# A transformer block on one core: background work of ScalarE and VectorE is put elsewhere, with six smaller edits

## The chip, the cores and the metric

The kernel runs on one core of one Trainium2 chip. The metric is the time of one execution on the device in microseconds (us). An engine is called by the profile's short name where a row is meant: PE is TensorE (matmuls), PEld its weight loads, DVE VectorE, ACT ScalarE, POOL GpSimd, SP SyncE. Engines run in parallel, each through its own list of instructions in order, and wait for each other by semaphores. A transfer is issued from the list of SP, ACT or POOL.

## The reference

One block of a transformer on x of 2048 tokens by 1024 features, all float32. `layernorm` has no weights.

```python
def attn(h):                       # h = layernorm(x)
    q, k, v = (h @ w.T + b for w, b in ((wq, bq), (wk, bk), (wv, bv)))
    q, k, v -> (tokens, 32 heads, 32)
    scores = einsum('shd,std->sht', q, k) / sqrt(32)     # heads of ONE token against each other
    return einsum('sht,std->shd', softmax(scores), v)

def ffn(h):                        # h = layernorm(x)
    dq1, dq2, dq3 = (nf4_quant_dequant(w) for w in (w1, w2, w3))   # blocks of 64, 16 levels
    return (silu(h @ dq1.T) * (h @ dq2.T)) @ dq3.T                 # 1024 -> 2752 -> 1024

x = x + attn(layernorm(x))
x = x + ffn(layernorm(x))
```

`nf4_quant_dequant` divides each block of 64 weights by its largest magnitude, replaces every value by the nearest of 16 levels, and multiplies by the magnitude again.

## The kernel before

**Products.** Every large product is a two by two block product done with seven multiplications instead of eight (Strassen's scheme in Winograd's form). A multiplication is `mm4`: four matmuls of 128x128 by 128x512, which the profile shows as eight rows. The scheme needs sums and differences of the blocks (`S1` to `S4` of the one side, `T1` to `T4` of the other), which VectorE makes, and reads a PSUM bank several times while it still grows: `copied` and the copies of `Unit` are ScalarE's copies of such a bank, and the next multiplication into the bank must wait for the copy.

**Stages.** The queries' sweep goes over eight pairs of token blocks (128 tokens each): `load_x`, `normed_x`, transposes into `A` (plain order) and `V` (order for the values) by TensorE with two ScalarE copies per PSUM tile, `products`, then `qk_T` adds the bias. The A and V operands are kept in DRAM. In the first pair the weight combinations T1 to T4 are made on the chip as the blocks land. The keys' sweep multiplies the same operands by the keys' weights and does `attend` (scores and softmax). The values' sweep multiplies by the values' weights and does `gather` (context), `residual` (adds x and normalizes) and `keep_T` (transposes the result, forms its sums and stores them). Then comes the feed-forward part: `Unit`s (gate and up projection of one block of 128 hidden features, for one of two halves of the tokens) in groups of four, and after each group `down7`, the sum over the group's hidden features. `down7` copies each PSUM bank with ScalarE (`acc`) and adds it to `x1d` in DRAM with accumulating transfers of GpSimd. The last groups go through `down`.

**The background.** The quantization of w1, w2, w3 is 64 jobs, a generator (`background`) that runs beside all of this. A job loads a weight block `wn`, finds the blocks' maxima (`absmax`, which also divides: `scaled` with `rc`), walks through 15 steps that build `r` (twelve of them are an `sg` on ScalarE, L242, and an operation on VectorE, L243; two buffers of `sg`), multiplies by the maxima (`scaled` with `wa`), and is transposed by TensorE, copied by ScalarE (`finish`, L162) and stored (`wd`). Jobs of kind "1" and "2" are the up side, "3" the down side. `scaled` on ScalarE is one small instruction for each of 16 blocks of 64 columns.

**What sets the order.** The main program calls `advance(n)` to emit n background pieces, `flush` to emit a finished job's transposes, and, in the feed-forward part, `spent(us)`, which emits `us * RATE` pieces (RATE is 0.69 a microsecond). `until(kind, c)` emits whatever is missing of a job that is needed now. TensorE's order is exactly that of the program. The other engines' order is made by a scheduler from the emitted instructions, unless `tc.issue_after` puts an instruction behind another. `hook["scale"]` says which engine does the last `scaled` of a job: in the sweeps "ACT"; from the feed-forward part on "DVE", which means VectorE for even jobs and ScalarE for odd ones.

Of the kernel before, what the change touches and what calls it, by code (L numbers as in the profile page):

```python
# [69 lines left out]
def preln_block_kernel(  # L70
# [41 lines left out]

    def mean_var(pool, src, dst):
        st = pool.tile([P, 2, 6], FP, tag="st", name="st")
        for j in range(2):
            nc.vector.bn_stats(st[:, j, :], src[:, ts(j, 512)])
        nc.vector.bn_aggr(dst, st.rearrange("p a b -> p (a b)"))
# [74 lines left out]
    def scaled(dst, src, by, nb):  # L192

        for n in range(nb):
            nc.scalar.mul(dst[:, ts(n, BLOCK)], src[:, ts(n, BLOCK)], by[:, n : n + 1])  # L195
# [4 lines left out]
    def absmax(kind, c, wn):  # L200

        w = width(kind, c)
        nb = w // BLOCK
        v = wn[:, :w]
        am = fs.tile([P, 16], FP, tag="am", name="am")
        rc = fs.tile([P, 16], FP, tag="rc", name="rc")[:, :nb]
        nc.vector.tensor_reduce(  # L207
            am[:, :nb],
            v.rearrange("p (b e) -> p b e", e=BLOCK),
            AX.X,  # L210
            ALU.max,
            apply_absolute_value=True,
        )
        nc.vector.scalar_tensor_tensor(rc, am[:, :nb], 0.0, am[:, :nb], ALU.is_equal, ALU.add)
        nc.vector.reciprocal(rc, rc)  # L215
        scaled(v, v, rc, nb)
        return am

    def background():
# [4 lines left out]
        for n, (kind, c) in enumerate(jobs):  # L224
# [7 lines left out]
            for i, (side, edge, code) in enumerate(STEPS):  # L232
# [6 lines left out]
                else:  # L239
                    t = dqp.tile([P, E], FP, tag="sg", name="sg")[:, :w]  # L240
                    by = BIG if side == "+" else -BIG
                    nc.scalar.activation(t, v, AF.Copy, bias=-edge * by, scale=by)  # L242
# [6 lines left out]
            if hook["scale"] == "ACT" or n % 2:  # L249
                scaled(r, r, wa, w // BLOCK)  # L250
            else:
                r3 = r.rearrange("p (b e) -> p b e", e=BLOCK)
                f = wa[:, : w // BLOCK].unsqueeze(2).to_broadcast([P, w // BLOCK, BLOCK])
                nc.vector.tensor_tensor(r3, r3, f, ALU.mult)
# [68 lines left out]
    def load_bias(b, nm):  # L323
        t = wpool.tile([P, 32], FP, tag=nm, name=nm)
        for g in range(4):
            nc.scalar.dma_start(t[g * 32 : (g + 1) * 32, :], b)
        return t
# [24 lines left out]
    def products(A, fill, used=lambda name: None, apart=None):  # L352
# [7 lines left out]
        def copied(nm, src):  # L360
            t = pair.tile([P, TB], FP, tag=nm, name=nm)
            nc.scalar.copy(t, src)  # L362
            return t
# [21 lines left out]
        if apart is None:  # L385
            mul(z, S4, "B22", False, True)
            nc.scalar.copy(ce[:, 512:], z)
# [68 lines left out]
    xt = {}  # L456

    def load_x(i):
        xt[i] = work.tile([P, E], FP, tag="x", name="xt", bufs=2)
        for n in range(2 if i == 0 else 1):  # L460
            cols = ts(n, TB) if i == 0 else slice(None)
            nc.sync.dma_start(xt[i][:, cols], xf[ts(i, P), cols])
# [3 lines left out]
    def normed_x(i):  # L466
        xn = work.tile([P, E], FP, tag="xn", name="xn", bufs=2)
        return normed(xt.pop(i), xn, opening if i < 2 else None)

    class Inputs:  # L470
# [11 lines left out]
        def transposes(self, j):  # L482
            for half in range(2):
                pt = ps_t.tile([P, 4, P], FP, tag="pt", name="pt")
                for k in range(4):
# [4 lines left out]
                nc.scalar.copy(  # L490
                    v.rearrange("p k (c m) -> p k c m", c=4),
                    pt.rearrange("p k (m c) -> p k c m", c=4),
# [16 lines left out]
    qb_sb, kb_sb, vb_sb = (load_bias(b, nm) for b, nm in ((qb, "qb"), (kb, "kb"), (vb, "vb")))  # L509
# [9 lines left out]
    with tc.issue_after(three(nxt.A, nxt.a21).ins):  # L519
# [40 lines left out]
    for p in range(NP):  # L560
# [11 lines left out]
        def fill(n):  # L572
# [5 lines left out]
            with nullcontext() if p else tc.issue_after(opened):  # L578
                advance(0 if n == 5 else 1)
# [17 lines left out]

    sweep, sweep_at = ExitStack(), ExitStack()
# [85 lines left out]
    def residual(i, at, x1):  # L684
# [6 lines left out]
        nc.vector.tensor_tensor(x1, x1, cx, ALU.add)  # L691
        for n in range(2):
            nc.sync.dma_start(x1d[i][n], x1[:, ts(n, TB)])
        return normed(x1, x1)
# [26 lines left out]
    even = {}  # L721

    def keep_T(i, x1n):

        t = work.tile([P, 2, 4, P], FP, tag=f"xT{i % 2}", name="xT")
        for half in range(2):
# [3 lines left out]
            nc.scalar.copy(t[:, half], pt)  # L730
# [11 lines left out]
        for n in range(4):  # L742
            u[n + 1] = work.tile([P, 4, P], FP, tag="xU", name="xU", bufs=2)
# [4 lines left out]
    for p in range(NP):  # L748
# [9 lines left out]
        def fill(n):  # L758
            if n in (7, 2, 5, 4) and (p, n) != (1, 7):
                part()  # L760
            advance(2 if n == 6 else 1)
# [25 lines left out]
    hook["scale"] = "DVE"  # L787
# [124 lines left out]
    class Unit:  # L912
# [9 lines left out]
        def mul(self, n, dst, start, stop):  # L922
            mm4(dst, self.w[:, self.A[n]], op(self.B[n], self.tbp), start, stop)
            spent(3.43)
# [90 lines left out]
    def down7(g, tbp, sides):  # L1015
# [4 lines left out]
        turn = [0]  # L1020

        def mul(n, dst, q, start, stop):
# [10 lines left out]
            spent(1.71, turn[0] % 2 == 0)  # L1033
# [7 lines left out]
        for first in (0, 2):  # L1041
# [31 lines left out]
            for n, k in opening + [  # L1073
# [3 lines left out]
                p(n, k)  # L1077

# [132 lines left out]
```

## Time and profile before

| | |
|---|---|
| median of 3 runs (lowest, highest) | 2480.15 us (2476.73, 2480.97) |
| the profiled execution, its span | 2484.77 us, 2483.0 us |
| mean granted clock of TensorE | 0.989 |
| busy: PE, DVE, ACT, POOL | 96%, 80%, 65%, 11% |
| 12.4 to 240 us (queries' sweep): PE, DVE, ACT busy of 227.6 us | 211.3, 218.0, 125.9 us |
| 240 to 528 us (keys' sweep): of 288 us | 279.1, 233.5, 137.7 us |
| 528 to 835 us (values' sweep): of 307 us | 283.5, 271.2, 139.9 us |
| a step on ScalarE (L242), on VectorE (L243), 128x1024 | 1060 ns, 1221 ns |
| a small scale on ScalarE (L195), 1032 of them | 341 ns each, 267.5 us together |
| a scale of a whole tile on VectorE (L254) | 1218 ns |

A busy share says how long an engine worked, not whether anybody waited for it. A row of the timeline gives the start, the length, the engine, the line, the operation with its tiles and shape, how many such instructions follow each other, and in brackets how long the engine stood idle before it and what ended that. Eight rows of 128x512 matmuls at full rate print as 3.60 us, though the next eight start 3.43 us later, since a matmul's end overlaps the next one's start. A granted clock under 1.00 in a stretch means that TensorE ran part of it at a lower rate.

### The profile page before, as it was taken

What the parts mean: (1) busy time and instruction counts of PE and PEld (TensorE: products, weight loads), DVE (VectorE), ACT (ScalarE), POOL (GpSimd) and SP (SyncE); (2) the same over time, 40 slices, a digit from 0 to 9 for tenths busy, and PEclk for the clock granted to TensorE, in tenths of its full rate; (3) what the DMA queues carried; (4) which work ended last, traced back from release to release, by engine and by line L of the source; (5) the groups of instructions that cost most, each with busy time, mean ns of one, the idle gap of its engine ahead of it and who ended that gap; (6) DMA issues with size and microseconds to landing.
All of it is one profiled execution on the core that took longest, in us unless ns stands there. A gap on an engine that the chain in (4) does not pass through costs nothing.

```text
span 2483.0 us, 36752 instructions
## 1 busy us (share of the span) xinstructions
PE 2389.2 (96%) x14000; PEld 1117.1 (45%) x14000; DVE 1981.2 (80%) x2211; ACT 1610.2 (65%) x3267; POOL 278.4 (11%) x352
## 2 busy tenths in 40 slices
PE   7999999999899999999999999999999999999998
PEld 4444455545445444444444444444444444444433
DVE  8999688879988597889989899898998988871022
ACT  3566544344554278898887888889889798881200
POOL 0010000000000012030120301203012030020300
PEclk9999999999999999999999999999999999999999
DMA  8888543666669588384883948739577394872983
GB/s 310 301 295 339 214 154 125 228 221 216 198 234 317 196 299 172 126 183 156 310 186 114 185 163 289 181 140 183 165 280 173 132 206 159 278 159 88 173 310 122
DMA packets 179745, 513.90 MB, mean 207 GB/s; under 512 B 16176, under 2 KB 70448, under 8 KB 157168
## 3 DMA queue, kind: packets, MB, share of 16 engines
q1 hardware_dynamic: 138672, 438.08, 48.5%
q0 software_dynamic: 40320, 73.42, 18.4%
q8 instruction: 110, 1.80, 0.3%
q14 instruction: 67, 0.55, 0.1%
q10 hardware_dynamic: 576, 0.05, 0.0%
HBM read 283.69 MB, written 227.80 MB: 206 GB/s over the span
## 4 chain that ended last, share of the span: by engine, by line
issue 25%; ACT 13%; DVE 13%; PE 11%; DMA 6%; POOL 1%; DVEq 0%; POOLq 0%; ACTq 0%
DVE r L243 8%; DMA x1d<-acc 5%; ACT sg L242 4%; PE z L343 4%; ACT wn L195 4%; ACT acc L1037 2%; ACT r L195 2%; PE z L1024 2%; PE q L343 2%; PE po L1104 1%; POOL x1d L1039 1%; PE po L1115 1%; PE y L1024 1%; PE rr L343 1%; ACT wop L162 1%
## 5 line engine op out<-in xcount | busy, mean ns | idle before, releaser
L243 DVE SCALAR_TENSOR_TENSOR r<-sg,r 128x1024 f32<-128x1024 f32 x780 | 945.3, 1213 | 104.1 <-ACT sg L242 72.7
L242 ACT ACTIVATE sg<-wn 128x1024 f32<-128x1024 f32 x780 | 812.6, 1053 | 309.6 <-DVE r L243 294.0
L1039 POOL DMA_DIRECT2D x1d<-acc x280 | 243.0, 887 | 1282.1 <-ACT acc L1037 1138.4
L343 PE MATMUL z<-xB,w 128*128 128x512 f32 x720 | 324.6, 599 | 5.6 <-ACT u L944 3.8
L343 PE MATMUL z<-xT,w 128*128 128x512 f32 x656 | 298.1, 597 | 4.6 <-ACT u L937 4.3
L343 PE MATMUL q<-xT,w 128*128 128x512 f32 x656 | 291.6, 592 | 0.0
L195 ACT ACTIVATE wn<-wn,rc 128x64 f32<-128x64 f32 x1032 | 267.5, 341 | 19.1 <-DVE rc L215 19.1
L1024 PE MATMUL z<-w,h 128*128 128x512 f32 x496 | 233.6, 599 | 9.4 <-ACT acc L1037 6.5
L343 PEld LDWEIGHTS z<-xB,w 128*128 128x128 f32 x720 | 134.6, 191 | 173.6 <-issue 153.0
L343 PEld LDWEIGHTS z<-xT,w 128*128 128x128 f32 x656 | 122.4, 191 | 154.4 <-issue 137.0
L343 PEld LDWEIGHTS q<-xT,w 128*128 128x128 f32 x656 | 123.3, 190 | 149.5 <-issue 146.9
L343 PE MATMUL z<-wT,A 128*128 128x512 f32 x384 | 178.2, 607 | 2.9 <-ACT g L362 2.5
L343 PE MATMUL q<-wT,A 128*128 128x512 f32 x384 | 174.5, 598 | 2.5 <-DVE wT L522 2.5
L343 PE MATMUL z<-wB,A 128*128 128x512 f32 x320 | 153.9, 626 | 12.8 <-ACT u L362 12.8
L195 ACT ACTIVATE r<-r,am 128x64 f32<-128x64 f32 x608 | 154.8, 342 | 14.6 <-DVE r L243 14.3
L1024 PE MATMUL y<-w,h 128*128 128x512 f32 x320 | 150.4, 594 | 1.3 <-DVE h L1003 1.1
L343 PE MATMUL rr<-xB,w 128*128 128x512 f32 x328 | 147.5, 592 | 0.0
L1024 PEld LDWEIGHTS z<-w,h 128*128 128x128 f32 x496 | 92.1, 191 | 121.7 <-issue 96.7
L207 DVE TENSOR_REDUCE am<-wn 128x16 f32<-128x1024 f32 (+1 forms) x65 | 78.3, 1204 | 54.5 <-ACT r L195 54.2
L1037 ACT COPY acc<-z 128x512 f32<-128x512 f32 x160 | 92.9, 580 | 36.9 <-PE z L1024 26.3
L343 PEld LDWEIGHTS q<-wT,A 128*128 128x128 f32 x384 | 72.6, 192 | 90.5 <-issue 85.4
L343 PEld LDWEIGHTS z<-wT,A 128*128 128x128 f32 x384 | 71.5, 193 | 83.0 <-issue 78.1
(132 smaller groups left out, 2585.8 us busy)
## 6 DMA issues: line engine op xcount, KB each, us to landing
x1d<-acc POOLq DMA_DIRECT2D x280, 256.0 KB, 6.4
wd<-wop SPq DMA_DIRECT2D x31, 2048.0 KB, 7.5
w<-wd SPq DMA_DIRECT2D x41, 1280.0 KB, 7.8
wn<-in_w_dram SPq DMA_DIRECT2D x63, 512.0 KB, 5.0
xT<-xdT SPq DMA_DIRECT2D x28, 1024.0 KB, 9.2
xB<-xdB SPq DMA_DIRECT2D x24, 1024.0 KB, 9.0
w<-wd SPq DMA_DIRECT2D x42, 512.0 KB, 5.0
w<-wd SPq DMA_DIRECT2D x10, 1536.0 KB, 7.6
```

The lines of the kernel that those rows point to most:

```text
L162: nc.scalar.copy(o[:q, first + half], pt[:q])
L195: nc.scalar.mul(dst[:, ts(n, BLOCK)], src[:, ts(n, BLOCK)], by[:, n : n + 1])
L207: nc.vector.tensor_reduce(am[:, :nb], v.rearrange("p (b e) -> p b e", e=BLOCK), AX.X, ALU.max, apply_absolute_value=True,)
L242: nc.scalar.activation(t, v, AF.Copy, bias=-edge * by, scale=by)
L243: nc.vector.scalar_tensor_tensor(r, t, code, r, ALU.min, ALU.max)
L343: nc.tensor.matmul(dst, w[:, k, :], xop[:, k, :], start=start and k == 0, stop=stop and k == 3, skip_group_check=True,)
L1024: nc.tensor.matmul(dst, side[n][:, ts(q, P)], w3T[g[2 * m]][:, W3[n]], start=start and m == 0, stop=stop and m == 1, skip_group_check=True,)
L1037: nc.scalar.copy(t, src)
L1039: nc.gpsimd.dma_start(x1d[8 * tbp + 2 * q + j][n], t, accum_op=ALU.add)
L1104: nc.tensor.matmul(po, hs[c][j][:, ts(q, P)], w3T[c][:, ts(n, 512)], start=(c == g[0]), stop=False, skip_group_check=True,)
L1115: nc.tensor.matmul(po, hs[NFULL][r, ts(q, P)], w3T[NFULL][r, ts(n, 512)], start=False, stop=True, skip_group_check=True,)
```

## The change

Seven things change at once.

1. In the queries' and the values' sweep some ScalarE copies are marked, and the background instructions of ScalarE named by `urgent["rule"]` (small scales; in the values' sweep also the steps) are issued behind the last one that is marked. Behind the sweeps the rule is empty.
2. `scaled` takes an engine. In `down7` all scales are VectorE's, those of `absmax` too. Elsewhere in the feed-forward part ("both") the last scale is ScalarE's for even jobs and VectorE's for odd ones.
3. The biases are loaded by GpSimd, behind the normalization of the second token block, instead of by ScalarE at the start.
4. The second pair's tokens are loaded behind the first operand sums, and the first block's normalization comes before the second block's.
5. The residual is formed in the context's tile `cx` and stored from there; the normalized result goes to `x1`.
6. The third buffer of `xU`.
7. The advances: three fewer in the first pair of the queries' sweep, another distribution in the values' sweep, `spent(3.3)` for 3.43 in a unit and `spent(1.85)` for 1.71 in `down7`.

```diff
+    urgent = {"last": None, "rule": ()}
+    def marked(ins):
+        urgent["last"] = ins.ins
+    def behind(kind):
+        last = urgent["last"]
+        return tc.issue_after(last) if last and kind in urgent["rule"] else nullcontext()
...
-    def scaled(dst, src, by, nb):
-        for n in range(nb):
-            nc.scalar.mul(dst[:, ts(n, BLOCK)], src[:, ts(n, BLOCK)], by[:, n : n + 1])
+    def scaled(dst, src, by, nb, engine):
+        if engine == "DVE":
+            d, s = (a.rearrange("p (b e) -> p b e", e=BLOCK) for a in (dst, src))
+            f = by[:, :nb].unsqueeze(2).to_broadcast([P, nb, BLOCK])
+            nc.vector.tensor_tensor(d, s, f, ALU.mult)
+            return
+        with behind("scale"):
+            for n in range(nb):
+                nc.scalar.mul(dst[:, ts(n, BLOCK)], src[:, ts(n, BLOCK)], by[:, n : n + 1])
...
-        scaled(v, v, rc, nb)
+        scaled(v, v, rc, nb, "DVE" if hook["scale"] == "DVE" else "ACT")
...
-                    nc.scalar.activation(t, v, AF.Copy, bias=-edge * by, scale=by)
+                    with behind("step"):
+                        nc.scalar.activation(t, v, AF.Copy, bias=-edge * by, scale=by)
...
-            if hook["scale"] == "ACT" or n % 2:
-                scaled(r, r, wa, w // BLOCK)
-            else:
...
+            engine = ("ACT", "DVE")[n % 2] if hook["scale"] == "both" else hook["scale"]
+            scaled(r, r, wa, w // BLOCK, engine)
...
-            nc.scalar.dma_start(t[g * 32 : (g + 1) * 32, :], b)
+            nc.gpsimd.dma_start(t[g * 32 : (g + 1) * 32, :], b)
...
-            nc.scalar.copy(t, src)
+            marked(nc.scalar.copy(t, src))
...
-            nc.scalar.copy(ce[:, 512:], z)
+            marked(nc.scalar.copy(ce[:, 512:], z))
...
+    urgent["rule"] = ("scale",)
...
+        if i == 2:
+            tc.add_manual_dep(
+                load.ins,
+                opening["first"].name,
...
+        with tc.issue_after(hook["normed"]) if i == 1 else nullcontext():
+            return normed(xt.pop(i), xn, opening if i < 2 else None)
...
-                nc.scalar.copy(
-                    v.rearrange("p k (c m) -> p k c m", c=4),
-                    pt.rearrange("p k (m c) -> p k c m", c=4),
+                marked(
+                    nc.scalar.copy(
+                        v.rearrange("p k (c m) -> p k c m", c=4),
+                        pt.rearrange("p k (m c) -> p k c m", c=4),
+                    )
...
-    qb_sb, kb_sb, vb_sb = (load_bias(b, nm) for b, nm in ((qb, "qb"), (kb, "kb"), (vb, "vb")))
...
+    with tc.issue_after(opening["last"]):
+        qb_sb = load_bias(qb, "qb", work)
+        kb_sb = load_bias(kb, "kb", wpool)
+        vb_sb = load_bias(vb, "vb", wpool)
+    opening["first"] = three(nxt.A, nxt.a21).ins
...
-                advance(0 if n == 5 else 1)
+                advance(0 if n == 5 or p == 0 and n in (7, 6, 2) else 1)
...
+    urgent["rule"] = ()
...
-        nc.vector.tensor_tensor(x1, x1, cx, ALU.add)
+        nc.vector.tensor_tensor(cx, x1, cx, ALU.add)
         for n in range(2):
-            nc.sync.dma_start(x1d[i][n], x1[:, ts(n, TB)])
-        return normed(x1, x1)
+            nc.sync.dma_start(x1d[i][n], cx[:, ts(n, TB)])
+        return normed(cx, x1)
...
+    urgent["rule"] = ("scale", "step")
...
-            nc.scalar.copy(t[:, half], pt)
+            marked(nc.scalar.copy(t[:, half], pt))
...
-            u[n + 1] = work.tile([P, 4, P], FP, tag="xU", name="xU", bufs=2)
+            u[n + 1] = work.tile([P, 4, P], FP, tag="xU", name="xU", bufs=3)
...
-            advance(2 if n == 6 else 1)
+            advance({7: 2, 6: 2, 5: 1, 3: 2}.get(n, 0))
...
-    hook["scale"] = "DVE"
+    hook["scale"] = "both"
+    urgent["rule"] = ()
...
-            spent(3.43)
+            spent(3.3)
...
+        hook["scale"] = "DVE"
...
-            spent(1.71, turn[0] % 2 == 0)
+            spent(1.85, turn[0] % 2 == 0)
...
+        hook["scale"] = "both"
```

More of the change, by code (lines that the diff above doesn't have):

```diff
@@ L248, in background @@
                     yield
-            if hook["scale"] == "ACT" or n % 2:
-                scaled(r, r, wa, w // BLOCK)
-            else:
-                r3 = r.rearrange("p (b e) -> p b e", e=BLOCK)
-                f = wa[:, : w // BLOCK].unsqueeze(2).to_broadcast([P, w // BLOCK, BLOCK])
-                nc.vector.tensor_tensor(r3, r3, f, ALU.mult)
+            engine = ("ACT", "DVE")[n % 2] if hook["scale"] == "both" else hook["scale"]
+            scaled(r, r, wa, w // BLOCK, engine)
             pending.append(finish(kind, c, r))
@@ L321, in load_W, with load_bias @@
         nc.sync.dma_start(new_w(name), src)
-    def load_bias(b, nm):
-        t = wpool.tile([P, 32], FP, tag=nm, name=nm)
+    def load_bias(b, nm, pool):
+        t = pool.tile([P, 32], FP, tag=nm, name=nm)
         for g in range(4):
-            nc.scalar.dma_start(t[g * 32 : (g + 1) * 32, :], b)
+            nc.gpsimd.dma_start(t[g * 32 : (g + 1) * 32, :], b)
         return t
@@ L461, in load_x @@
             cols = ts(n, TB) if i == 0 else slice(None)
-            nc.sync.dma_start(xt[i][:, cols], xf[ts(i, P), cols])
+            load = nc.sync.dma_start(xt[i][:, cols], xf[ts(i, P), cols])
+        if i == 2:
+            tc.add_manual_dep(
+                load.ins,
+                opening["first"].name,
+                mybir.DependencyInfo(
+                    mybir.DependencyClass.Sync, mybir.DependencyReason.DATA
+                ),
+                reason="the first weights come first",
+            )
     opening = {}
@@ L467, in normed_x @@
         xn = work.tile([P, E], FP, tag="xn", name="xn", bufs=2)
-        return normed(xt.pop(i), xn, opening if i < 2 else None)
+        with tc.issue_after(hook["normed"]) if i == 1 else nullcontext():
+            return normed(xt.pop(i), xn, opening if i < 2 else None)
     class Inputs:
@@ L489, in transposes @@
                 nc.scalar.copy(a, pt)
-                nc.scalar.copy(
-                    v.rearrange("p k (c m) -> p k c m", c=4),
-                    pt.rearrange("p k (m c) -> p k c m", c=4),
+                marked(
+                    nc.scalar.copy(
+                        v.rearrange("p k (c m) -> p k c m", c=4),
+                        pt.rearrange("p k (m c) -> p k c m", c=4),
+                    )
                 )
@@ L518, in preln_block_kernel @@
     new_w("T3"), new_w("T2"), new_w("T4")
-    with tc.issue_after(three(nxt.A, nxt.a21).ins):
+    with tc.issue_after(opening["last"]):
[3 more added lines that the diff above has]
+    opening["first"] = three(nxt.A, nxt.a21).ins
+    with tc.issue_after(opening["first"]):
         for n in range(2):
```

## The prediction

> **What bounds the kernel now.** I read the page first, then the waits by total time, busy time by stage, and the timeline around each stretch in which TensorE stood still.
>
> ```profile
> PE 2389.2 (96%) x14000; PEld 1117.1 (45%) x14000; DVE 1981.2 (80%) x2211; ACT 1610.2 (65%) x3267; POOL 278.4 (11%) x352
> ```
>
> TensorE is busy for 2389.2 of 2483.0 us, so the same matmuls can win only its 94 idle us, and the time in which it runs below its full rate. The full rate is seen in the timeline: eight rows of 128x512 (four matmuls) start 3.43 us apart from the next eight, and print as 3.60. The windows view by stage, TensorE alone, shows where it is not reached (stretch, length, busy time, count, granted clock, DMA share, GB/s):
>
> ```profile
> 34.50:48.60 14.10, 8.06 (x25) 0.76 0.78 289
> 621.00:636.00 15.00, 10.73 (x156) 0.77 0.47 154
> 673.00:729.00 56.00, 56.00 (x1027) 1.00 0.83 277
> 729.00:742.00 13.00, 8.87 (x148) 0.87 0.29 93
> 766.00:835.00 69.00, 60.37 (x1044) 0.93 0.87 291
> 835.00:2380.00 1545.00, 1513.94 (x3803) 1.00 0.68 190
> ```
>
> The reader is to see that the loss lies in a few short stretches of the queries' sweep (12 to 240 us) and the values' sweep (528 to 835 us), while 673 to 729 us, the same work without a stop, loses nothing; and that where TensorE stops, its granted clock falls too. The feed-forward part loses 31 us in 1545. The timeline tells what the stops wait for. Two of them, and what ScalarE (ACT) did before:
>
> ```profile
> 35.19 3.93 ACT L195 ACTIVATE wn<-wn,rc 128x64 f32<-128x64 f32 x16
> 39.02 0.57 ACT L489 COPY A<-pt 128x512 f32<-128x512 f32 x1
> ...
> 42.03 1.11 PE L486 MATMUL pt<-ident,xn 128*128 128x128 f32 x4 [6.04 <-ACT V L490]
> 42.94 5.87 PE L343 MATMUL y<-wB,A 128*128 128x512 f32 x8
> ...
> 624.29 1.06 ACT L242 ACTIVATE sg<-wn 128x1024 f32<-128x1024 f32 x1 [6.03 <-DVE r L243]
> 625.62 1.06 ACT L242 ACTIVATE sg<-wn 128x1024 f32<-128x1024 f32 x1 [0.27 <-DVE r L243]
> 626.95 1.06 ACT L242 ACTIVATE sg<-wn 128x1024 f32<-128x1024 f32 x1 [0.27 <-DVE r L243]
> 627.91 0.57 ACT L362 COPY u<-z 128x512 f32<-128x512 f32 x1
> 628.53 6.69 PE L343 MATMUL z<-wB,A 128*128 128x512 f32 x8 [4.27 <-ACT u L362]
> ```
>
> In both, a copy out of PSUM that TensorE needs stands on ScalarE behind background work of the weights' quantization: sixteen scales (3.93 us), or three steps `sg`, each of which waits for VectorE (DVE). In the feed-forward part, the nine sums with background beside them (`down7`) and the eight stretches of units between them:
>
> ```profile
> sum 476.40, PE 457.51 PEld 202.53 DVE 388.63 ACT 423.46 POOL 195.97; mean PE 50.83 PEld 22.50 DVE 43.18 ACT 47.05 POOL 21.77
> sum 818.10, PE 806.45 PEld 363.02 DVE 746.96 ACT 680.75 POOL 20.28; mean PE 100.81 PEld 45.38 DVE 93.37 ACT 85.09 POOL 2.53
> ```
>
> In the sums ScalarE is the fuller one (0.89 busy, VectorE 0.82) and TensorE idles for 18.9 us; in the units VectorE is (0.91, ScalarE 0.83) and TensorE idles for 11.6 us.
>
> **The change part by part.** Gains and losses are against the profiled execution, 2484.8 us (span 2483.0 and 1.8 around it), which is 4.6 above the median of the runs.
>
> *Biases and second tokens.* Twelve loads (0.45 us issue each) leave ScalarE's queue for GpSimd's, behind the second token block's `rs`. In both programs' order every load waits for the earlier user of one of eight completion semaphores, and ScalarE's and SyncE's loads share these. So the query weights were held back by the biases: B11 was issued at 3.94, B22 at 7.05, T1 at 7.47 us, and T1 landed at 17.6; VectorE waited for it 2.67 us, TensorE 2.51:
>
> ```profile
> 18.98 5.40 PE L343 MATMUL q<-wT,A 128*128 128x512 f32 x8 [2.51 <-DVE wT L522]
> ```
>
> After, the first eight loads of SyncE find free semaphores and can be issued by about 0.7 + 8 x 0.45 = 4.3 us. T1 is the end of 4.2 MB; in the trace the queue moved about 290 GB/s while it ran dry between issues and 390 to 420 when full (13 to 23 us), with some 2.3 us from a byte's start to the landing. From 1.9 us that is 14.3 to 18.7; I take 15.5. Then `q` starts at about 16.8 instead of 18.98, and VectorE's chain of six operations after T1 (7.2 us) sets the next product. The stop cost 2.51 idle and 1.80 slow (5.40 against 3.60): 4.3; I take a gain of 2.5, bounds 0 and 4.5. Normalizing x0 before x1's statistics saves nothing more, as T1 is last. The second tokens now wait for the first `S2` (about 15 us, before: issued at 11.97); the two weight blocks `wn` pass them on SyncE's queue, the bytes ahead of them stay the same, and their first reader is at 25.4 us: 0.
>
> Here a rule speaks against the change. The Trainium skill, "DMA: Bandwidth & Descriptors", section "SWDGE vs HWDGE vs iDMA", says that plain transfers belong on SP or ACT and that GpSimd's are slower, since software writes their descriptors. The nearest row, GpSimd's `x1d<-acc`, takes 887 ns to issue and 6.4 us to land: 12 x 0.887 = 10.6 us of GpSimd's queue from about 9.5 us; its next work was at 27.43, and VectorE first read a bias at 52.97. So slower loads cost 0. By the rule alone the biases would be no gain and the sum below 26.0 instead of 28.5.
>
> *The queries' sweep.* Scales go behind the last copy that the code marks. In the new order the four A copies of the second pair have no scale before them (before: 3.92 us); the row above loses 6.04 idle and 5.87 - 3.60 = 2.27 slow. What stays is 16 copies' pace (0.48 us each) and VectorE's operand differences, some 1.3 us: gain 7, bounds 3 and 8.3. Three background steps of the first pair go to later pairs. The six other stops at transposes were 1.36, 2.59, 0.34, 0.74, 0.34 and 2.36 us idle, and 1.70 slow after the last: 9.4. But the background directly before the `u` copies, which the A copies follow, sums in the new order to 37 us where it was 36; two of its blocks are now 7.1 us long. I take 3, bounds -4 and 8.
>
> At these slow rows the skill's clock rule weighs in ("TensorE: Matmul & The Clock Gate", section "What's actually happening": the clock halves after an idle window of about 3.4 us, a free-running one, and is back after as long a busy one). The trace has slow rows after idle times of 2.51 and 2.36 us, and none after 2.59 or 1.36. By the rule read as a threshold, 1.80 and 1.70 here and 1.80 after a 3.29 us stop below would not come from the stops, and my sum would be some 3.5 us less; I go by the rows.
>
> *The keys' sweep.* No line of it changes; the background arrives three or four steps later. Its one large stop (2.46 idle, 6.48 - 3.60 slow) may go or double: 0, bounds -5 and 5.
>
> *The values' sweep.* Steps too now follow the marked copies, and advances move from the fills around the products T1 and T4 to those after T3 and S4. Three stops at `u`: 4.27, 3.29 and 4.13 us idle, rows of 6.69, 5.40 and 5.37 against 3.60, so 11.7 + 6.7 = 18.4 us. Before `u2` and `u4` the old order had six, five and six steps there, the new order has before each at most two, or one and 16 scales (1.06 + 3.9 = 5.0 us; TensorE works 8.2 us between the two copies). I take 14, bounds 7 and 18. The residual is built in `cx` and stored from there, so the normalization no longer waits for the store (`DVE x L337 <- DMA x1d<-x`, 11.1 us in all); the next transpose into `cx` waits for it instead, 13 us later, where a store lands in 5 to 7. `xU` has a third buffer (waits of 11.2 us in all). Both are VectorE waits, most at 660 to 840 us; of TensorE's 8.6 idle us in 766 to 835 I take 3, bounds -5 and 8.
>
> *The sums.* `scale` is "DVE" in `down7`, "both" elsewhere with the parities exchanged. In all 456 small scales leave ScalarE, 28.5 blocks of 16 at 0.257 us (267.5 us / 1032 plus its kin): 117 us; VectorE gets 29 operations 128x1024 more, by the row L254 (1218 ns) 34.6 us. `spent(1.85)` brings 8% more background into the sums, 3.3 brings 4% less into the units. ScalarE in the sums: 423 - 117 + 17 = 323 of 476, 0.68. VectorE: 389 + 35 + 29 = 453 of 476, 0.95; in the units 0.91 to 0.89. TensorE idled 18.9 us in the sums; 2.9 of these were a weight load and about 4 accumulating stores whose buffers were not free (`ACT acc L1037 <- DMA x1d<-acc`, 13.9 us on ScalarE). Of the other 12 I take 8, bounds -10 and 13.
>
> *What comes late.* The background is three to six steps behind. In the fifth group the transposes of the last down block now stand 3.4 us of TensorE work later and both halves together. There the load was already late:
>
> ```profile
> 2152.61 4.54 PE L1024 MATMUL z<-w,h 128*128 128x512 f32 x6 [2.90 <-DMA w<-wd]
> ```
>
> From the second half's transposes (2134.37) to the landing were 18.2 us, of which 8.4 the store; after, some 13 us of TensorE's work lie in between: loss 4, bounds 0 and 10. In the units the work before the PSUM copies grows from 385 to 422 us over 164 copies: loss 1. For stops that a fuller VectorE makes in the sums I take 4, an estimate of under half a us in each of the nine.
>
> Sum: 2.5 + 7 + 3 + 0 + 14 + 3 + 8 = 37.5, less 4 + 1 + 4 = 9: 28.5. The profiled execution would be 2456.3; less the 4.6 to the median, 2452.
>
> **The rivals.** *VectorE becomes the bound of the sums* (slower). My 0.95 counts durations; dependent steps start 1.33 us apart where they last 1.21, and ScalarE's steps wait for VectorE, so accumulator copies behind them wait too. It decides where the demand passes 1.0: each per cent over is 0.53 us in each of nine sums, 4.7 us. At 1.09 that is 43 us, and with the 28 of the other parts the kernel is 15 slower than before: 2495. For it: 209 waits of `sg` on `r` in the feed-forward part (142 us). Against it: VectorE itself waited there 72 us for `sg` and 44 us for the scales, which leave ScalarE.
>
> *The stops move on.* The copies are no longer behind scales, but behind what VectorE delivers late, above all in the queries' sweep, where VectorE is 0.96 busy (218.0 of 227.6 us). Then 7 of the first 12.5, 7 of the 17 in the values' sweep and 4 of 8 stay, 18, less 9: 9 faster, 2471.
>
> *The order does nothing* for lack of marked copies where it counts: only the loads, the first pair (whose order is seen) and the residual work, 12.5, less 9: 2477.
>
> **How the numbers follow.** A measurement of this kernel can tell about 0.2%, 5 us. The likeliest case, 0.68: 2452, by itself 2437 to 2466. Stops move on, 0.16: 2466 to 2475. No difference (the third rival, or gains and losses that cancel), 0.05: 2475 to 2485. VectorE as bound, 0.11: above 2485. So faster 0.84, same 0.05, slower 0.11. The range 2437 to 2475 leaves out 0.16 above and some 0.04 below.
>
> **What would show it.** In the profile after: `q` of the first pair near 17 us with an idle time under 1 us; no stop of 6 us at 42 us; rows of 3.60 after the `u` copies of the values' sweep and a granted clock of 0.95 or more in 621 to 636; ScalarE near 0.7 and VectorE near 0.95 busy in the sums; a wait for `w<-wd` of 4 to 9 us near 2125. Wrong would be: no gap between VectorE's steps in the sums and accumulator copies late behind `sg`, or stops as long as before at other copies in the two sweeps.

## The result: 0.84% slower, and the profile after

The changed kernel takes 2502.9 us (median of 6, 2499.55 to 2503.47) where the kernel before took 2480.99: a ratio of 1.0084, 95% interval 1.0073 to 1.0095. The forecast was 2452. The profiled execution took 2503.03 us, its span 2501.2, which is 18.2 longer than that of the profiled execution before (which was 3.8 above its median, so the medians differ by 21.9). The page's first part shows that the work moved as the change says:

```profile
PE 2389.0 (96%) x14000; PEld 1116.9 (45%) x14000; DVE 2018.6 (81%) x2239; ACT 1511.8 (60%) x2811; POOL 285.0 (11%) x364
```

ScalarE has 456 instructions and 98 us less, VectorE 28 and 37 us more, TensorE the same 14000 and the same busy time (2389.2 before). Slow rows count as busy, so the 18 us are net idle time of TensorE, and the next question is where.

The 13480 matmuls that are not transposes of quantized weights come in the same order in every kernel of this study. So I took the start of the same matmul in each trace, and cut the span there. "Opening" ends at the matmul that started at 47.2 us in the kernel before (in the first pair's last products), the next marks are those at 240, 528 and 835 us (the ends of the sweeps), then the first of the nine sums; "sums" adds these nine and "units" what follows each of them; the tail is the last group. A row adds up to some 0.4 us more than its span. Times in us; "late" is how many background steps the first pair of the queries' sweep leaves out without their being done again before the feed-forward part.

| kernel | late | median | ratio to before (95%) | opening | queries' | keys' | values' | to sums | sums | units | tail |
|---|---|---|---|---|---|---|---|---|---|---|---|
| before | 0 | 2480.99 | 1 | 47.2 | 193.1 | 287.7 | 307.6 | 74.7 | 476.6 | 917.8 | 178.7 |
| after | 3 | 2502.9 | 1.0084 (1.0073 to 1.0095) | 36.7 | 198.1 | 293.4 | 316.5 | 74.7 | 487.0 | 918.5 | 176.8 |
| x1_values_old | 3 | 2502.18 | 1.0073 (1.0058 to 1.0087) | 37.4 | 198.1 | 292.2 | 314.1 | 75.3 | 487.2 | 921.1 | 176.8 |
| x2_values_norule | 3 | 2499.15 | 1.0059 (1.0045 to 1.0073) | 37.9 | 197.0 | 292.0 | 311.5 | 75.7 | 487.2 | 918.6 | 176.8 |
| y1_values_resid_old | 3 | 2502.14 | 1.0089 (1.0076 to 1.0102) | 37.5 | 198.1 | 293.1 | 310.4 | 77.3 | 486.7 | 919.3 | 176.8 |
| x3_sums_old | 3 | 2494.22 | 1.0044 (1.0030 to 1.0058) | 37.3 | 197.7 | 291.4 | 317.5 | 74.7 | 479.5 | 918.6 | 176.8 |
| x4_sums_scales | 3 | 2504.82 | 1.0083 (1.0069 to 1.0097) | 37.5 | 197.6 | 295.1 | 317.2 | 74.7 | 487.6 | 920.8 | 176.8 |
| y4_sums_pace | 3 | 2497.21 | 1.0069 (1.0057 to 1.0081) | 37.6 | 199.2 | 292.5 | 314.3 | 74.7 | 484.0 | 913.5 | 178.2 |
| y3_q_norule | 3 | 2495.73 | 1.0067 (1.0055 to 1.0079) | 38.0 | 199.1 | 288.4 | 314.7 | 74.7 | 483.9 | 918.1 | 176.8 |
| y2_q_advances | 0 | 2477.04 | 0.9989 (0.9983 to 0.9996) | 43.3 | 192.1 | 294.0 | 300.9 | 76.6 | 476.7 | 912.7 | 178.6 |
| z4_two_late | 2 | 2486.0 | 1.0010 (1.0002 to 1.0018) | 43.6 | 190.7 | 291.4 | 305.1 | 75.8 | 487.4 | 911.5 | 178.3 |
| z3_four_late | 4 | 2496.83 | 1.0053 (1.0039 to 1.0067) | 37.8 | 198.9 | 295.6 | 308.8 | 76.1 | 486.4 | 914.6 | 178.5 |
| z1_back_pair2 | 0 | 2482.54 | 1.0002 (0.9994 to 1.0010) | 37.0 | 205.4 | 293.6 | 302.9 | 75.1 | 477.6 | 913.4 | 176.8 |
| z2_back_keys | 0 | 2477.06 | 0.9981 (0.9972 to 0.9989) | 37.4 | 195.9 | 294.6 | 302.0 | 76.1 | 478.0 | 914.1 | 176.8 |
| w4_before_skip | 3 | 2497.33 | 1.0058 (1.0046 to 1.0070) | 37.6 | 198.9 | 292.8 | 310.6 | 74.7 | 482.8 | 919.5 | 178.7 |
| w3_noskip_values_old | 0 | 2482.69 | 1.0001 (0.9993 to 1.0010) | 44.8 | 191.5 | 291.7 | 310.1 | 74.3 | 479.3 | 912.8 | 176.8 |
| v2_before_resid | 0 | 2483.68 | 1.0007 (0.9997 to 1.0016) | 46.8 | 192.0 | 287.6 | 308.0 | 74.7 | 473.5 | 918.3 | 178.7 |
| w1_best | 0 | 2472.31 | 0.9968 (0.9957 to 0.9979) | 37.3 | 197.9 | 288.6 | 303.4 | 74.8 | 478.7 | 911.6 | 178.4 |
| w2_best_pace | 0 | 2473.21 | 0.9960 (0.9947 to 0.9973) | 37.2 | 198.2 | 290.3 | 302.7 | 75.2 | 476.8 | 914.2 | 176.8 |
| v1_best_resid_old | 0 | 2479.51 | 0.9988 (0.9981 to 0.9995) | 37.6 | 199.4 | 290.2 | 306.8 | 80.4 | 479.2 | 912.6 | 176.8 |

The medians of before in the five later comparisons were 2479.8 to 2483.3, so the ratio, not the median, compares two rows. The stages are one profile each. The queries' sweep has the same source in eight of the kernels (after, x1, x2, x3, x4, y1, y4, z2) and takes 195.9 to 199.2 us; the keys' sweep, the same in seven of these (without z2), takes 291.4 to 295.1. So two rows that differ by less than 4 us in one sweep are not told apart. The sums agree better: in four kernels with the same feed-forward code and the same late steps (after, x1, x2, y1) they differ by 0.5. The rows that carry the argument are y2 (the skipped steps given back), z1 and z2 (the steps done later) and w4 (the skip as the only edit).

Read the second row against the first. The opening won 10.5 us, and every stage up to the sums gave something back: 5.0, 5.7, 8.9, then 10.4 in the sums. Two stretches of the timeline after show how TensorE waits in the values' sweep. First, near 551 and 583 us (start, length, engine, line, operation; idle before and releaser in brackets):

```profile
549.15 2.01 ACT L260 ACTIVATE sg<-wn 128x1024 f32<-128x1024 f32 x2
550.25 1.23 DVE L261 SCALAR_TENSOR_TENSOR r<-sg,r 128x1024 f32<-128x1024 f32 x1 [3.08 <-ACT sg L260]
551.39 1.93 DVE L432 STREAM_TRANSPOSE vd<-ce 128x1024 f32<-128x1024 f32 x1
553.20 1.87 DVE L432 STREAM_TRANSPOSE vd<-co 128x1024 f32<-128x1024 f32 x1
...
556.21 1.47 PE L457 MATMUL cx<-vd,pl 32*32 32x32 f32 x128 [4.14 <-DVE vd L435]
...
582.88 3.93 ACT L212 ACTIVATE r<-r,am 128x64 f32<-128x64 f32 x16 [2.25 <-DVE r L261]
583.52 1.91 PE L172 MATMUL ptw<-ident,r 128*128 128x128 f32 x4 [3.25 <-ACT r L212]
...
585.22 4.65 PE L357 MATMUL z<-wT,A 128*128 128x512 f32 x8
```

A step `sg` stands behind the marked copy `u`; its partner on VectorE stands in front of VectorE's transposes of the values and waits 3.08 us, and TensorE, which needs those, 4.14. Thirty us later a job's last scales are ready only when TensorE already stands at that job's transposes. The second stretch is the last token block:

```profile
829.52 1.20 DVE L261 SCALAR_TENSOR_TENSOR r<-sg,r 128x1024 f32<-128x1024 f32 x1
830.64 1.20 DVE L723 TENSOR_TENSOR cx<-x,cx 128x1024 f32<-128x1024 f32 x1
831.76 1.21 DVE L261 SCALAR_TENSOR_TENSOR r<-sg,r 128x1024 f32<-128x1024 f32 x1
832.89 1.28 DVE L127 BATCH_NORM_STATS2 st<-cx 128x6 f32<-128x512 f32 x2
834.08 1.21 DVE L261 SCALAR_TENSOR_TENSOR r<-sg,r 128x1024 f32<-128x1024 f32 x1
...
837.31 1.94 PE L762 MATMUL pt<-ident,x 128*128 128x128 f32 x8 [5.57 <-DVE x L351]
...
839.04 5.74 PE L357 MATMUL z<-xB,w 128*128 128x512 f32 x8
```

Three background steps, 3.6 us, stand between the links of the chain that TensorE waits for. Before, the same chain had none of them (the background was between two jobs there), and TensorE waited 0.98 us:

```profile
831.32 1.06 PE L729 MATMUL pt<-ident,x 128*128 128x128 f32 x8 [0.98 <-DVE x L337]
```

### The profile page after: what moved, and what is told of

Same layout as the page of the kernel before. It is cut to its first block, busy times and chain, and to the rows that moved or that the text cites. A ratio compares the mean times of both kernels' runs of the same rounds, so it can differ in the third digit from the quotient of the medians.

```text
span 2501.2 us, 36350 instructions
## 1 busy us (share of the span) xinstructions
PE 2389.0 (96%) x14000; PEld 1116.9 (45%) x14000; DVE 2018.6 (81%) x2239; ACT 1511.8 (60%) x2811; POOL 285.0 (11%) x364
## 4 chain that ended last, share of the span: by engine, by line
DVE 29%; issue 18%; PE 15%; ACT 8%; DMA 5%; POOL 1%; DVEq 0%; SPq 0%; POOLq 0%; ACTq 0%
DVE r L261 16%; PE z L357 5%; DMA x1d<-acc 3%; ACT sg L260 3%; PE z L1059 2%; ACT wn L212 2%; DMA wd<-wop 2%; ACT r L212 2%; PE q L357 2%; PE po L1140 1%; DVE r L253 1%; PE y L1059 1%; DVE vd L432 1%; DVE am L224 1%; DVE r L255 1%
## 5 line engine op out<-in xcount | busy, mean ns | idle before, releaser
L212 ACT ACTIVATE wn<-wn,rc 128x64 f32<-128x64 f32 x728 | 186.5, 341 | 9.3 <-DVE rc L232 9.3
L357 PE MATMUL z<-wT,A 128*128 128x512 f32 x384 | 183.4, 622 | 5.5 <-ACT u L376 3.3
L357 PE MATMUL z<-wB,A 128*128 128x512 f32 x320 | 148.1, 606 | 0.3 <-ACT u L376 0.2
L212 ACT ACTIVATE r<-r,am 128x64 f32<-128x64 f32 x456 | 114.2, 338 | 16.5 <-DVE r L261 16.4
L974 DVE TENSOR_TENSOR g<-g,rr 128x512 f32<-128x512 f32 x41 | 27.9, 681 | 96.6 <-PE rr L357 96.6
```

Source lines behind the costliest of these rows:

```text
L357: nc.tensor.matmul(dst, w[:, k, :], xop[:, k, :], start=start and k == 0, stop=stop and k == 3, skip_group_check=True,)
L974: nc.vector.tensor_tensor(self.g0, self.g0, r, ALU.add)
```

## The experiments

**Undoing parts, at first of the values' sweep and the sums.** My first theory was that the rule itself costs, as the rows at 550 us suggest. x1 takes out rule and advances of the values' sweep, x2 the rule alone:

```diff
     even = {}
-    urgent["rule"] = ("scale", "step")
-            advance({7: 2, 6: 2, 5: 1, 3: 2}.get(n, 0))     # x1 only
+            advance(2 if n == 6 else 1)                     # x1 only
```

> The changed kernel (2502.9 us) with the values' sweep as it was: no rule there for what follows the marked copies, and the old advances (2 after S3, else 1). Theory A (on ScalarE the rule puts steps and scales behind copies that wait for TensorE, while VectorE's partner operation and the transposes of the weights keep their places, so that VectorE or TensorE waits at those): the values' sweep, 315 us in the changed kernel and 307 before, comes back to 304 to 308, and the kernel to 2491 to 2496. Rival B (the sweep is longer because the background arrives late from the queries' sweep): the sweep stays at 312 or more, the kernel within 3 us of 2503. Rival C (the residual in cx and the third xU buffer cost it): as B.

> The changed kernel with the values' sweep without the rule, but with the new advances (two after T1, S3 and S4, one after T2). Theory A (the rule is what costs): the sweep at 304 to 309 us, the kernel 2491 to 2497. Rival D (the advances bunch the background in pairs, and the rule matters little): the sweep at 312 to 318 us, the kernel within 3 us of 2503 or above.

The theory fell with x1: 2.4 us of the sweep's 8.9, and nothing that the time can tell. The stops at `u`, which the change had removed, came back in their old size, three of them with 4.36 or 4.37 us idle, and slow rows behind each (eight in 6.4 or 6.5 us; the last row here is cut off by the window; x1, timeline):

```profile
626.76 1.06 ACT L260 ACTIVATE sg<-wn 128x1024 f32<-128x1024 f32 x1 [1.94 <-DVE r L261]
628.09 1.06 ACT L260 ACTIVATE sg<-wn 128x1024 f32<-128x1024 f32 x1 [0.27 <-DVE r L261]
629.05 0.57 ACT L376 COPY u<-z 128x512 f32<-128x512 f32 x1
...
629.67 2.93 PE L357 MATMUL z<-wB,A 128*128 128x512 f32 x3 [4.37 <-ACT u L376]
```

So the rule does what it says, and yet the sweep is as long. x2 won 5.0 us in the sweep, half of what was expected, and 0.25% of the time; against x1 its sweep is not told apart.

> The changed kernel with the scales in the sums shared by ScalarE and VectorE again, and the old pace (3.43 and 1.71). The nine sums take 487.7 us in the changed kernel and 477.1 before. Theory E (scales on VectorE together with more background in the sums bring the sums' operations closer, so that they wait for the buffers of the accumulating stores and of the stored weights): sums at 476 to 482 us, the kernel 2493 to 2498. Rival F (the ten us come from the background's lag, the late w3 load first of all): sums at 485 to 490, the kernel within 3 us of 2503.

> The changed kernel with the scales in the sums shared by ScalarE and VectorE again, but the new pace (1.85 and 3.3). Theory E1 (the pace alone makes the sums longer): sums at 486 to 500 us, the kernel 2502 to 2515, since ScalarE gets its scales back and still has 8% more background. Theory E2 (the scales on VectorE make them longer): sums at 476 to 482, the kernel 2493 to 2498.

x3 undoes engine and pace of the sums, x4 the engine alone (`hook["scale"] = "DVE"` taken out; `spent` back in x3). x3 brings 7.5 us back, x4 none. Later y4 undid the pace alone:

> The changed kernel with the old pace (3.43 and 1.71), and the scales of the sums on VectorE as changed. The sums took 487.0 us with both new, 479.5 with neither, 487.6 with the new pace alone. Theory P (the pace is what costs, the engine of the scales is worth little): sums at 474 to 481 us, the kernel 2492 to 2498. Rival (either alone costs as much as both): sums at 484 to 490 us, the kernel 2499 to 2505.

It wins 3.0 of the sums, which is the rival's range (484 to 490), though the time is in the theory's. So neither edit is the whole: with the scales where they were, the new pace costs 8.1 us of the sums (x4 against x3); with the old pace, the engine alone costs 4.5 (y4 against x3); both together cost 7.5.

**The residual, with the values' sweep all old.** y1 is x1 with the residual back in `x1` and two `xU` buffers.

> The values' sweep all as before: no rule, old advances, and also the residual in x1 and two xU buffers. With rule and advances undone the sweep was still 314.1 us (307.6 before). Rival C (the residual in cx or the third xU buffer cost the rest): the sweep at 306 to 309 us, the kernel 6 to 8 us below that run (2502.2). Rival B (the background stands in another phase, by five or so steps since the queries' sweep): the sweep at 312 us or more, the kernel 2500 to 2505.

The sweep came out another 3.7 shorter, between the ranges of both rivals, the stretch behind it 2.0 longer, and the kernel stayed at 1.0089. By the time, rival B (the phase of the background, that is, which of its steps meets which product) held, which the next runs test directly.

**The three skipped steps.** y2 gives the first pair its three background steps back, y3 takes the queries' rule out.

```diff
-                advance(0 if n == 5 or p == 0 and n in (7, 6, 2) else 1)     # y2
+                advance(0 if n == 5 else 1)                                   # y2
-    urgent["rule"] = ("scale",)                                               # y3
```

> The changed kernel with the first pair's three background steps given back (as before, one advance at each filling but that after S4). Rival B (a background late by those steps lengthens what follows): queries' sweep after the first pair 193 to 196 (198.1), keys' 287 to 291 (293.4), values' 308 to 313 (316.5), in all 10 to 18 us less, 2485 to 2493, with the opening two or so longer. Against it: each of those within 2 us of the changed kernel, the kernel 2500 to 2506.

> The changed kernel without the rule in the queries' sweep (new advances kept). If the rule wins where it was seen, at 42 us, and loses later by longer blocks before the A copies: opening up to the first y 36.7 back to 41 to 44, the rest of the sweep 198.1 down to 193 to 195, net 0 to +3. If the rule only wins: opening 41 to 44, rest 198 or more, kernel 2507 to 2511.

y2 is the key: 2477.0 us, 0.9989. The same kernel with three steps more in its first 43 us is 26.7 us shorter in span (0.95% by the two ratios, some 24 us): the opening 6.6 longer, but the queries' sweep 6.0, the values' 15.6, the sums 10.3 and the units 5.8 shorter. It gained more than was expected of it (2485 to 2493). Busy time, granted clock and DMA of the values' sweep, after and in y2 (windows view; stretch, length, then PE, PEld, DVE, ACT, POOL, PEclk, DMA share, GB/s):

```profile
528.50:843.50 315.00, 285.92 (x4870) 150.01 (x4871) 276.25 (x297) 145.96 (x293) 16.38 (x32) 0.96 0.70 235
...
529.40:830.30 300.90, 280.48 (x4893) 148.53 (x4887) 276.22 (x296) 142.04 (x289) 20.40 (x32) 0.97 0.72 245
```

VectorE has the same 276 us of work in both. TensorE idles 29.1 us in the one and 20.4 in the other, and is 5.4 us longer busy, which is slow rows. After, it waits in this sweep 6.3 us for a job's last scales, 4.1 for `vd` and 4.9 for `co` of VectorE; in y2 2.2, 0.9 and 2.1. The stop at the last token block is not part of the difference: in y2 three steps stand in that chain too, and TensorE waits 6.04 us.

```profile
824.59 1.94 PE L762 MATMUL pt<-ident,x 128*128 128x128 f32 x8 [6.04 <-DVE x L351]
```

y2 also shows what had removed the stop of the first pair. Both timelines there, after first:

```profile
31.47 0.59 ACT L376 COPY u<-z 128x512 f32<-128x512 f32 x1 [6.28 <-PE z L357]
...
31.95 1.57 ACT L514 COPY A<-pt 128x512 f32<-128x512 f32 x3
...
34.06 0.66 PE L511 MATMUL pt<-ident,xn 128*128 128x128 f32 x4 [1.32 <-ACT V L516]
```

```profile
31.64 0.59 ACT L376 COPY u<-z 128x512 f32<-128x512 f32 x1 [6.28 <-PE z L357]
...
32.13 3.92 ACT L212 ACTIVATE wn<-wn,rc 128x64 f32<-128x64 f32 x16
...
35.96 0.56 ACT L514 COPY A<-pt 128x512 f32<-128x512 f32 x1
...
38.95 1.11 PE L511 MATMUL pt<-ident,xn 128*128 128x128 f32 x4 [6.04 <-ACT V L516]
```

With the steps there and the rule in force, the sixteen scales stand as before, directly behind the marked `u` copy and in front of the A copies, since those are written later in the program; the stop of 6.04 us is back to the hundredth. y3, without the rule, has the short stop:

```profile
35.38 0.66 PE L509 MATMUL pt<-ident,xn 128*128 128x128 f32 x4 [1.32 <-ACT V L514]
```

So the gain at 42 us is the skip's, and the rule had no part in it. Both expectations for y3 took the gain for the rule's (an opening of 41 to 44 us without it) and were wrong: the opening is 38.0, and the kernel came out faster, at 2495.7. What the rule does instead is seen in y3's keys' sweep, 288.4 where it is 293.4: TensorE waits 0.6 us there for the copies `u` and `g`, where it waits 5.4 after.

**Is it lateness, or where the steps fall?** z4 skips two steps, z3 four; z1 and z2 skip three and do them in the second pair, or in the keys' first pair.

```diff
+  advance(0 if n == 5 or p == 0 and n in (7, 6) else 1)                                      # z4
+  advance(0 if n == 5 or p == 0 and n in (7, 6, 2, 3) else 1)                                # z3
+  advance(0 if n == 5 or p == 0 and n in (7, 6, 2) else 2 if p == 1 and n in (7, 6, 2) else 1)  # z1
+  advance(2 if p == 0 and n in (7, 6, 2) else 1)          # z2, in the keys' fillings
```

> The changed kernel; the first pair's three background steps stay away, and the second pair does them beside its own (two after T1's predecessors S3, S2 and SA12 each). From the third pair on the background stands where it stood with the steps never skipped (2477.0 us). Theory L (what the skipped steps cost is where the background stands in the later stages): opening 36 to 38 us, the rest of the queries' sweep 195 to 200, keys' 292 to 295, values' 299 to 303, sums 475 to 479, units 911 to 915, and the kernel 2470 to 2479. Against it (the first pair's empty fillings themselves matter): values' and sums as in the changed kernel, 314 and 485 or more, the kernel 2497 or more.

> As the run before, but the three steps are done in the keys' first pair, where VectorE has room. Theory L: opening 36 to 38, queries' rest 197 to 199, keys' 290 to 296, values' 299 to 303, sums 475 to 479, the kernel 2471 to 2481. Against it: values' and sums as in the changed kernel, 2497 or more.

> The changed kernel with a fourth step taken from the first pair (after S4 also). If lateness is what costs (26 us for three steps): some 5 to 10 us more, 2508 to 2513. If it is the phase, that is which steps meet which products, the cost need not grow: each later stage changes by several us in either direction, and the kernel may lie anywhere from 2480 to 2510.

> The changed kernel with two steps taken from the first pair (after S3 and S2), not three. If lateness is what costs: between the run with none skipped and the changed kernel, 2490 to 2500. If it is the phase: anywhere from 2475 to 2510, and stages not in between (values' outside 301 to 316 us or sums outside 477 to 487).

z1 and z2 settle that the first pair's empty fillings themselves cost nothing, only where the background stands later: with the steps made up, values' sweep (302.9, 302.0) and sums (477.6, 478.0) are those of y2 (300.9, 476.7). Making them up in the second pair costs 7.3 us there, which took z1 out of its expected range (2482.5, not 2470 to 2479); in the keys' sweep it costs 1.2, less than two rows can tell. z3 and z4 split the rest. The values' sweep over 0, 2, 3 and 4 late steps is 300.9, 305.1, 316.5, 308.8, and the kernel 2477, 2486, 2503 and 2497 us: neither grows steadily, so where the steps fall counts, not only how many are late. The ninth sum is another thing: 54.9 us with none late, 61.8, 59.1 and 62.3 with two, three and four. That is a deadline, and its row names it (after; in y2, with the steps on time, it is the last row of the second fence):

```profile
2152.20 0.60 PE L172 MATMUL ptw<-ident,r 128*128 128x128 f32 x4
...
2156.04 0.65 PE L172 MATMUL ptw<-ident,r 128*128 128x128 f32 x4 [3.24 <-ACT wop L173]
...
2160.20 0.32 SPq L191 DMA_DIRECT2D wd<-wop  x1
...
2167.03 0.32 SPq L843 DMA_DIRECT2D w<-wd  x1
...
2175.03 2.93 PE L1059 MATMUL z<-w,h 128*128 128x512 f32 x3 [7.18 <-DMA w<-wd]
```

```profile
2145.60 0.70 PE L1059 MATMUL z<-w,h 128*128 128x512 f32 x1 [1.90 <-DMA w<-wd]
```

**The skip alone in the kernel before, and the values' edits on time.** Four runs more.

> The kernel before, with one edit: the first pair skips the three background steps. If lateness costs in any kernel: opening 40 to 42 (47.2), values' 312 to 320 (307.6), sums 480 to 487 (476.6), the kernel 2484 to 2500. If it cost only together with the other edits: values' and sums within 3 us, the kernel 2472 to 2478.

> The changed kernel with no step skipped (2477.0 us), and the values' sweep without the rule and with the old advances. If these two are worth what the forecast had (14 us): values' sweep 312 to 317 instead of 300.9, kernel 2488 to 2494. If they are worth only what the stage shows against the kernel before (6.7 us, residual and xU among it): values' sweep 304 to 309, the kernel 2479 to 2486.

w4 is the kernel before with the skip as its only edit: 1.0058, its span 12.3 us longer, although its opening is 9.6 shorter. Here the loss lies in the queries' sweep (5.8), the keys' (5.1) and the sums (6.2); the values' sweep, expected at 312 to 320, is 3.0 longer, less than two rows can tell. The ninth sum is 62.6 us there, TensorE waiting 9.96 for the load:

```profile
2166.30 4.26 PE L1024 MATMUL z<-w,h 128*128 128x512 f32 x6 [9.96 <-DMA w<-wd]
```

w3 prices rule and advances of the values' sweep where the background is on time: 310.1 without, 300.9 with them, 9.2 us. Part of it is lost elsewhere: the spans differ by 6.4 us and the ratios by 0.12%, 3 us. With three steps late the same two edits were worth nothing in the sweep (316.5 against x1's 314.1).

**Better versions.** w1 is z2 without the queries' rule, w2 is w1 with the old pace, v1 is w1 with the old residual and `xU`; v2 is the kernel before with the residual in `cx` alone.

> The changed kernel, the three skipped steps done in the keys' first pair (2477.1 us so), and no rule in the queries' sweep. If that rule is what lengthens the keys' sweep (293.4 us with it, 288.4 without, at the late background): keys' 287 to 290 instead of 294.6, the rest as with the rule, the kernel 2468 to 2474. If the 5 us came from the phase: keys' 292 to 297, the kernel 2474 to 2481.

> As w1, with the old pace in the sums and units (3.43 and 1.71). If the new pace costs something of itself (8 us were seen at the late background): sums 470 to 475 instead of 478, 4 to 8 us under w1. If it only cost because the background was late: sums within 3 us of w1's.

> The best version so far (2472.3 us: the three steps done in the keys' first pair, no rule in the queries' sweep), with the residual in x1 and two xU buffers as before. If these edits cost time: values' sweep 299 to 301 instead of 303.4, the kernel 2468 to 2471. If they win, as forecast: values' sweep 305 to 308, the kernel 2474 to 2478.

> The kernel before with one edit: the residual is built in cx and stored from there. If it costs time: values' sweep 309 to 312 (307.6), the kernel 2482 to 2486. If it wins, as forecast: 304 to 306, the kernel 2476 to 2479. If the sums of VectorE's waits only trade places: within 1 us.

w1 is at 0.9968 and w2 at 0.9960, both faster than both kernels, and not to be told apart: on time the new pace costs 1.9 us of the sums and wins 2.6 in the units, both less than two rows of a sweep can tell. If the new pace cost time of itself, w2 was expected 4 to 8 us under w1; it is not. The keys' sweep fell from 294.6 to 288.6 with the rule gone, as at the late background. v1 was a miss: taking residual and third buffer back loses (0.9988; 3.4 us in the values' sweep, 5.6 behind it, in a profile of the slowest of its 22 executions), where y1 had hinted that it wins. In the kernel before, the residual without the third buffer shows no difference (v2, 1.0007). Whether that is the phase or the buffer was not run.

## Why the prediction was wrong, by its own steps

*The step that failed* is in the queries' part: "Three background steps of the first pair go to later pairs." It got no price, and "the background arrives three or four steps later" got 0 in the keys' sweep and, in "What comes late", 4 us for one load. The runs put the skip at 26.7 us of the span net of its own 6.6 in the opening (after against y2; 24 by the ratios), and at 12.3 net in the kernel before (w4; 14 by the ratio). That is about half of the 51 us between forecast and result. Without it, the other edits give 2477.0, a gain of 0.11%, still far from 2452; so other terms were too large as well.

- *Biases and second tokens* (2.5, bounds 0 and 4.5): right, 3.8. T1 landed at 15.28 (15.5 forecast), `q` started at 16.65 (16.8) with no stop, and by 23 us of the trace before the kernel was 3.8 ahead.
- *First pair's scales* (7): right in size, 6.7, by the wrong cause; the skip did it, and y2 has the full stop with the rule.
- *Other stops of the queries' sweep* (3, bounds -4 and 8): lost 5.0, outside. On time they gained 1.0 (y2), less than two rows can tell.
- *Keys' sweep* (0, bounds -5 and 5): lost 5.7, and 6.3 with the steps on time, so not by lateness. Two pairs of runs put 5 to 6 us on the queries' rule (after and y3, z2 and w1), but w4, which has no rule and only the skip, stands at 292.8: it is not one cause. In y2 one wait is as long as the loss. It is for a load that TensorE does not wait for in the trace before, nor in the one after:

```profile
279.13 1.77 PE L443 MATMUL sc<-kd,ql 32*32 32x32 f32 x128 [6.75 <-DMA ql<-qD]
```

The queries of the first pair were loaded from 269.73 us there, from 258.68 before. The same wait is 4.0 us in w4 and 3.7 in y3. The forecast had no term for it.
- *Values' sweep* (14, bounds 7 and 18): the stops at `u` did go (granted clock 1.00 from 621 to 637 us). Worth 9.2 in the sweep on time, 3 to 6 in the kernel; late, other waits replaced them: the sweep as a whole lost 8.9. I had counted only what stands before the `u` copies, not what VectorE and the transposes of the weights would wait for.
- *Residual and xU* (3): together about 5 us in the best version (0.9988 against 0.9968); the residual alone none in the kernel before. So the size is not a property of the edit alone, or it is the buffer's.
- *The sums* (8, bounds -10 and 13): lost 10.4, of it 3.2 in the ninth; on time 0.1. Here is the view by stage over the nine sums and what ScalarE waited for from 843.5 to 2400 us (total, times, longest):

```profile
sum 487.70, PE 460.73 PEld 205.06 DVE 445.08 ACT 373.05 POOL 200.13; mean PE 51.19 PEld 22.78 DVE 49.45 ACT 41.45 POOL 22.24
```

```profile
ACT acc L1072 <- DMA x1d<-acc: 22.9, 12, 3.2
...
ACT wop L173 <- DMA wd<-wop: 15.3, 9, 3.2
```

ScalarE fell to 0.76 busy, not 0.68, and VectorE rose to 0.91, not 0.95: the forecast took 100 us net out of ScalarE's work in the sums (all 117 of the scales, less 17 of background), where it lost only 50 (423 to 373). So ScalarE was relieved, but TensorE's idle time grew from 18.9 to 27.0 us. ScalarE's copies `acc` now wait longer for buffers whose accumulating stores have not landed (13.9 us before), and `wop` for the store of the job before (0.8 before). But these two rows do not carry the loss: y2 has 15.1 us of the second with sums of 476.7; of the first, x1 has 14.7 with sums as long as after's (487.2), and w2 18.3 with sums of 476.8. Of TensorE's own waits from the first unit on, the one for the load grew by 4.3 us, the one for `wop` by 3.6 (4.1 to 7.7). What lengthened the other sums is open; more buffers were not tried.
- *What comes late* (4, up to 10): TensorE waited 4.3 us more for the load, and 3.24 at the transposes ahead of it: right in place, and within its bounds.

Of the rivals, "VectorE becomes the bound" is out: 0.91, not over 1, and `r` waited 49.3 us for `sg` where it had waited 72.4. "The stops move on" was right in kind, behind what VectorE delivers late, but at 2471 its forecast covers only 19 of the 51 us between forecast and result. "The order does nothing" holds for the queries' rule at the first pair's stop alone. That work moved out of the way of one stop must be done somewhere in the other 2400 us was not among the rivals at all.

Open: which position in the values' sweep costs how much. Four values over the number of late steps show that the count alone does not set it; the rows name the waits, but no run takes one wait alone away.

## What to carry to other kernels

When background work is spread by hand among stages that each have their own critical copies, leaving a little out at one place moves all of it, and the price shows hundreds of us later: make the work up again in the next stage with room, and price the remaining stages as they then stand. Test single edits at the old phase of the background as well, since an edit can be worth 9 us in its stage at one phase and nothing at another. And an order "behind the last marked copy" protects only the copies written before the work; those written after it are not ahead of it.

## What the runs showed of the hardware

Rows ran at half rate without idle time directly before them. In the timeline after, 32x32 matmuls stand between the stop and the slow row:

```profile
424.58 1.77 PE L443 MATMUL sc<-kd,ql 32*32 32x32 f32 x128 [1.36 <-issue]
426.28 5.40 PE L357 MATMUL z<-wB,A 128*128 128x512 f32 x8
```

The eight rows took 5.40 us instead of 3.60, some of them starting 0.85 us apart instead of 0.43, with a granted clock of 0.66 from 426 to 431 us, while the row at 34.56 us, with a stop of 1.32 us and four 128x128 transposes ahead of it, took its 3.60. Yet neither the idle time nor the small matmuls decide it: in the kernel before, the same place has the same small matmuls behind an equal stop, and full rate after them (granted clock 1.00 from 428 to 433 us).

```profile
426.65 1.75 PE L429 MATMUL sc<-kd,ql 32*32 32x32 f32 x128 [1.40 <-issue]
428.33 3.70 PE L343 MATMUL z<-wB,A 128*128 128x512 f32 x8
```

Nor does a longer stop always bring slow rows: behind the 3.24 us at 2156.04 in the timeline after, sixteen rows took 7.03 us, which is full rate.

```profile
2156.53 7.03 PE L357 MATMUL z<-xB,w 128*128 128x512 f32 x16
```

So the idle time right before a row does not tell in these traces whether the row will be slow; what does was not tested.
